# Spare transposes and products on TensorE at three waits of a Nyström attention and expert kernel

## The chip, the cores and the metric

The kernel runs on one core of one Trainium2 chip. The metric is the device time of one execution in microseconds (us); times of several runs are given as their median. Durations of single instructions come from one profiled execution, with times counted from the start of its span.

The engines are called here by what the profile calls them: PE is TensorE's matmuls, PEld its weight loads, DVE is VectorE, ACT is ScalarE, POOL is GpSimd, SP is the engine that issues DMAs.

## What is computed

The input x has 16 batches of 1024 rows with 256 columns. Each batch goes through two residual sublayers:

```
x = x + layernorm(attention(layernorm(x)))
x = x + layernorm(experts(layernorm(x)))
```

The attention has 16 heads of 16 columns and 64 landmarks, the means of 16 neighbouring rows:

```
kernel1 = softmax(Q K_l^T)        # 1024 x 64
kernel2 = softmax(Q_l K_l^T)      # 64 x 64
kernel3 = softmax(Q_l K^T)        # 64 x 1024
SV  = (kernel1 @ iterative_inv(kernel2)) @ (kernel3 @ V)
out = SV @ w_proj
```

`iterative_inv` makes six rounds of a polynomial iteration for the inverse. The expert layer reconstructs each batch with eight small networks, picks the expert with the least squared error for the whole batch, and adds that expert's two-layer adapter to a common linear layer. All of this is in 32-bit floats.

## The kernel before

Each batch is cut into stages that are Python generators: `stage_a` (normalized and transposed rows, Q, K, V, and kernel3 @ V), `stage_p` (kernel2 and its inverse, times the result of `stage_a`), `stage_c` (kernel1 times that, the projection, the first residual), `stage_d1` (the eight reconstructions and the choice) and `stage_d2` (the chosen adapter and the second residual). The stages of neighbouring batches are interleaved by hand: the string `ORDER` says which of five streams emits its next piece, and the engines' instruction streams keep that order. Each engine runs its instructions strictly in the order in which they were emitted, and waits on semaphores for others.

PSUM, the memory that matmuls write, is used as four buffers of two banks. `two_banks` (L135) hands out the next one by the string `PAIRS`, again by hand; the first instruction that writes a buffer waits until the last one that reads its former contents is done.

The places that the change touches:

- **`spare` (L154)** issues matmuls of a constant tile of ones, in bf16, into a buffer whose contents are overwritten later. In the kernel before, `turned_rows` calls it for the last batch (20 products of 512 columns) and `stage_d2` for the last batch (16 of 512).
- **Row maxima of kernel3, in `stage_a`.** `max_of` computes scores and takes their maxima on DVE (L556, eight reductions in batch 0); L624 and `in_parts` (L340 to L344) join them and split them into three bf16 parts in `maxima3`; L632 transposes that on PE into the PSUM tile `pm`, and L634 turns it into `mrow`. Then `weights` adds the negative maxima by a product (L567), computes the scores again (L578), and ACT takes the exponential (L588); `times_v` (L604) multiplies with V, and L612 and L614 sum up over the steps. Between these, DVE computes statistics and normalized rows of the next batch (L363, L347, L390). L743 and L751 belong to `stage_p`: the column sums of kernel2 and their maximum.
- **The end of `stage_a`.** L653 transposes the sums `ut` into the tile `pu`; L658 and L660 divide. In `stage_p`, POOL copies the result (L767), and the inverse's products follow in `product` (L698, tiles `pkv`, `pxl`, `pxq`), between them ACT copies (L780) and DVE operations (L762, L771, L783, L787); L793 copies the result into the block matrix `w_bd`.
- **Maxima of kernel1, in `stage_c`.** `max_of` (L823 on PE, L831 on DVE, split by POOL at L340 to L344) fills `maxima`; `max_rows` transposes it by four transposes (L853) into a PSUM tile `pm`, and ACT copies that to `mt` (L855). `weights` computes scores (L862), subtracts the maxima by a product with `mt` (L870) and takes exponentials (L880); `weighted` multiplies with `w_bd` (L891); `projected` is L926.
- **`turned_rows` (L396)** transposes normalized rows by L404, which ACT copies out at L405. At the end of the work, these come from batch 14's `stage_d1` while batch 15 is in `stage_c`.

`ident_b` is a 128x128 identity in bf16, `ones_b` a 128x128 tile of ones in bf16; both are made once at the start.

Of the kernel before, what the change touches and what calls it, by code (L numbers as in the profile page):

```python
# [16 lines left out]
P = 128  # L17
# [63 lines left out]
def kernel(  # L81
# [17 lines left out]
    nc = tc.nc  # L99
# [9 lines left out]
    E, _, R = wa_down.shape  # L109
# [13 lines left out]
    def middle(ap, n):  # L123

        return ap.unsqueeze(1).to_broadcast([ap.shape[0], n, ap.shape[1]])
# [4 lines left out]
    def rows32(p):  # L130
        return slice(32 * p, 32 * p + 32)
# [3 lines left out]
    def two_banks(shape, name, dtype=F32):  # L135
        return ps2 if isinstance(ps2, Nothing) else ps2.tile(shape, dtype, tag=f"ps2_{next(pairs)}", name=name)

    LAST = NB - 1
# [12 lines left out]
        return work.tile(shape, F32, tag=tag, name=name, bufs=bufs)  # L151


    def spare(dst, n):  # L154

        for _ in range(n):
            nc.tensor.matmul(dst, lhsT=ones_b, rhs=middle(ones_b, 4), start=True, stop=True)

    live = [{} for _ in range(NB)]

# [76 lines left out]
    ident_b = const.tile([P, P], BF16, name="ident_b")  # L237
    nc.vector.tensor_copy(ident_b, ident)
    ones_b = const.tile([P, P], BF16, name="ones_b")
# [115 lines left out]
    def go(name, follows):  # L355
        return name, follows
# [37 lines left out]
    def turned_rows(b, at, xn_of, xt):  # L394

        for h in range(NT // 4):  # L396
            yield go((at, b, "xt", h), [(at, b, "xn", h)])
            xn = xn_of(h)
            pt = two_banks([P, NC, 4, P], f"pt_{at}{b}_{h}")
            if b == LAST:  # L400
                spare(pt[:, 0], 20 if h == 0 else 0)
            for j in range(4):
                for k in range(NC):
                    nc.tensor.transpose(pt[:, k, j, :], xn[:, j, k * P : (k + 1) * P], ident)  # L404
            nc.scalar.copy(xt[:, :, h * 512 : (h + 1) * 512], pt.rearrange("p k j c -> p k (j c)"))  # L405
# [40 lines left out]
    def stage_a(b):  # L446
# [13 lines left out]
        for i, scale in enumerate((HD**-0.5, 1.0)):  # L460
            for c in range(NC):
# [8 lines left out]
                dst = (qt, kt)[i]  # L470
                pq = rows_split(f"pq_{b}_{i}_{c}")
                f0 = i * D + c * P
                for k in range(ND):
                    for g in range(4):
                        nc.tensor.matmul(  # L475
                            pq[g // 2][:, g % 2, 0 : N // 4],
                            lhsT=wqkv_sb[rows32(g), k, f0 : f0 + P],
                            rhs=turned[rows32(g), k],
                            start=(k == 0),
                            stop=(k == ND - 1),  # L480
# [11 lines left out]
        for t0 in range(0, NT, 4):  # L492
# [5 lines left out]
            for k in range(ND):  # L498
                for g in range(4):
                    nc.tensor.matmul(  # L500
                        pv[g // 2][:, g % 2, 0:D],
                        lhsT=turned[rows32(g), k, t0 // 4, :],
                        rhs=wqkv_sb[rows32(g), k, 2 * D : 3 * D],
                        start=(k == 0),
                        stop=(k == ND - 1),
# [123 lines left out]
        in_parts(nc.vector, lambda q: maxima3[:, :, q * NC : (q + 1) * NC], most, most)  # L629
        yield go(("a", b, "mrow"), [("a", b, "mcol")])  # L630
        pm = two_banks([P, P], f"pm3_{b}", BF16)
        nc.tensor.transpose(pm, maxima3.rearrange("x p j -> x (p j)"), ident_b)  # L632
        mrow = small.tile([P, NC, P], BF16, tag="mrow", name=f"mrow_{b}", bufs=1)
        nc.vector.tensor_tensor(mrow, middle(pm, NC), last(minus_pick, P), ALU.mult)  # L634
# [14 lines left out]
            ("a", b, "u"), [("a", b, "ut", i) for i in steps] + ([("p", b - 2, "kv0")] if b >= 2 else [])  # L649
        )  # L650
        pu = two_banks([P, NC, PC, 32], f"pu_{b}")
        for c in range(NC):
            nc.tensor.transpose(  # L653
                pu[:, c].rearrange("x p d -> x (p d)"), ut[:, c].rearrange("x r l -> x (r l)"), ident
            )
# [143 lines left out]
    def stage_c(b):  # L799
# [49 lines left out]
        def max_rows(n):  # L849

            pm = two_banks([P, 512], f"pm_{b}_{n}", BF16)
            for t in range(4):
                nc.tensor.transpose(pm[:, t * P : (t + 1) * P], maxima[:, t, :], ident_b)  # L853
            mt = work.tile([P, 512], BF16, tag="mt", name=f"mt_{b}_{n}", bufs=1)
            nc.scalar.copy(mt, pm)  # L855
            return mt
# [87 lines left out]
        max_of(0, 2)  # L944
        yield before_rows(0)
        mt = max_rows(0)
        po = None
        for n in range(NW):
            for c in range(NC):
                yield before_weights(n, c)  # L950
                es = weights(n, c, mt)
                if n + 1 < NW:
                    yield before_max(n + 1, 2 * c)
                    max_of(n + 1, 2 * c)
                elif c == 0:
                    yield from added(n - 1, *po)
                yield before_weighted(n, c)
                if c == 0:
                    svn = buf4k("yc", [P, ND, P], f"svn_{b}_{n}")
                weighted(n, c, es, svn)  # L960
            flat = svn.rearrange("p k c -> p (k c)")
            nc.vector.transpose(flat, flat)  # L962
            if n + 1 < NW:
                yield before_rows(n + 1)
                mt = max_rows(n + 1)
            po = yield from projected(n, svn)
# [150 lines left out]
    def stage_d2(b):  # L1117
# [3 lines left out]
        if b == LAST:  # L1121
            spare(pa[:, 0, :].rearrange("p (j c) -> p j c", j=4), 16)
# [62 lines left out]
    def streams():  # L1185
        ffn, alone = [stage_d1, stage_d2], NB - 2
        return [
            *(chain([stage]) for stage in (stage_a, stage_p, stage_c)),
            chain(ffn, [b for b in range(NB) if b != alone]),
            chain(ffn, [alone]),  # L1190
        ]
# [68 lines left out]
```

## Time and profile before

| what | us |
|---|---|
| median of 3 runs | 1929.07 (1927.91 to 1931.19) |
| the profiled execution's own time | 1931.63 |
| its span, first to last instruction | 1929.7 |
| PE busy | 1836.1 |
| DVE busy | 1511.2 |
| ACT busy | 1131.7 |
| POOL busy | 211.9 |

The profile is of one execution. Busy time of PE counts a matmul from its start to its modelled end, so overlapping matmuls are counted once. PEclk is the granted clock of TensorE as a share of its full speed; in the view that cuts the span into 40 slices it is given in tenths. The chain of waits goes back from the last instruction, at each step to what released it. In the timeline, each line has the start, the length, the engine, the line of the code, the operation, the tiles, the count, and in brackets how long the engine stood idle before and who ended that. In the view by stretches, each line has the stretch, its length, then busy time and number of instructions of PE, PEld, DVE, ACT and POOL, then PEclk, the DMA engines' share and GB/s.

### The profile page before, as it was taken

The page shows a single profiled execution, that of the slowest core. Times are in us where ns is not written, and L with a number is a line of the kernel's source. Part 1 is how long each engine was busy: PE and PEld are TensorE (multiplying, and loading weights), DVE is VectorE, ACT ScalarE, POOL GpSimd, SP SyncE. Part 2 cuts the span into 40 slices and gives each one's busy share as a digit, 9 for nine tenths or more (in the row PEclk, how much of TensorE's full clock was granted, in tenths as well). Part 3 has the DMA queues.
Part 4 walks back from the last instruction along what each step waited for, and adds up shares of the span by engine and source line. Part 5 has one row for each costly group of instructions (what it writes and reads, how often), then busy time and mean ns, then how long its engine had stood idle before and what let it go on. Part 6 is the DMA issues. An engine that isn't in the chain of part 4 may idle for free.

```text
span 1929.7 us, 81483 instructions
## 1 busy us (share of the span) xinstructions
PE 1836.1 (95%) x37175; PEld 1260.4 (65%) x37175; DVE 1511.2 (78%) x2805; ACT 1131.7 (59%) x2434; POOL 211.9 (11%) x423
## 2 busy tenths in 40 slices
PE   6789999999999999999999999999999999999898
PEld 5767678567585766858667575766758475756444
DVE  7687878877879787888878888788787877786664
ACT  1244755574846657474674847557484666666575
POOL 1001001001010100101101010100111010010101
PEclk9899999999999999999999999999999999999899
DMA  9011011102011110201102020110201110010101
GB/s 205 2 25 25 3 29 47 24 7 68 6 47 23 51 24 7 69 4 49 25 18 57 7 68 2 51 25 7 68 6 47 24 51 3 17 36 18 35 4 49
DMA packets 65767, 64.30 MB, mean 33 GB/s; under 512 B 9244, under 2 KB 65424, under 8 KB 65424
## 3 DMA queue, kind: packets, MB, share of 16 engines
q1 hardware_dynamic: 65424, 59.11, 11.8%
q8 instruction: 291, 4.77, 1.0%
q14 instruction: 52, 0.43, 0.1%
HBM read 42.32 MB, written 16.78 MB: 31 GB/s over the span
## 4 chain that ended last, share of the span: by engine, by line
PE 74%; ACT 11%; DVE 11%; issue 2%; POOL 1%; DMA 0%; SPq 0%; DVEq 0%; POOLq 0%; ACTq 0%
PE pq L475 12%; PE ph L999 10%; PE pr L1029 7%; PE pv L500 6%; ACT df L1040 6%; PE pf L1158 5%; PE po L926 4%; PE psv L891 4%; PE psct L862 3%; PE psc L823 3%; PE psm L547 3%; PE pxl L698 3%; DVE mx L556 2%; PE psc L578 2%; PE pxq L698 2%
## 5 line engine op out<-in xcount | busy, mean ns | idle before, releaser
L1040 ACT ACTIVATE df<-df,bd_sb 128x512 f32<-128x512 f32 x512 | 362.4, 711 | 72.0 <-DVE df L1037 71.9
L1037 DVE TENSOR_TENSOR df<-pr,xt_d 128x1024 f32<-128x1024 f32 x256 | 297.0, 1215 | 52.3 <-PE pr L1029 39.0
L475 PE MATMUL pq<-xa,wqkv_sb 32*128 32x256 f32 x4096 | 243.4, 381 | 15.1 <-DVE xa L390 15.0
L1029 PE MATMUL pr<-ht,wd_sb 64*64 64x512 f32 x2048 | 240.8, 597 | 1.7 <-ACT ht L1007 1.2
L999 PE MATMUL ph<-xt_d,wd_sb 128*128 128x512 f32 x512 | 236.5, 604 | 1.9 <-DVE most L831 1.2
L475 PEld LDWEIGHTS pq<-xa,wqkv_sb 32*128 32x128 f32 x4096 | 218.1, 186 | 27.7 <-DVE xa L390 15.0
L556 DVE TENSOR_REDUCE mx<-psm 128x2 f32<-128x1024 f32 x128 | 149.6, 1217 | 32.5 <-PE psm L547 32.2
L999 PEld LDWEIGHTS ph<-xt_d,wd_sb 128*128 128x128 f32 x512 | 92.1, 189 | 116.1 <-issue 95.1
L880 ACT ACTIVATE e<-psct 128x1024 f32<-128x1024 f32 x128 | 124.0, 1022 | 66.4 <-PE psct L870 66.2
L831 DVE TENSOR_REDUCE most<-psc 128x16 f32<-128x1024 f32 x128 | 150.2, 1216 | 13.5 <-PE psc L823 10.3
L1029 PEld LDWEIGHTS pr<-ht,wd_sb 64*64 64x64 f32 x2048 | 68.3, 132 | 126.1 <-issue 61.6
L588 ACT ACTIVATE e<-psc 128x1024 f32<-128x1024 f32 x128 | 123.0, 1026 | 31.4 <-PE psc L578 30.9
L1007 ACT ACTIVATE ht<-ph,bd_sb 128x1024 f32<-128x1024 f32 x64 | 70.9, 1108 | 105.3 <-PE ph L999 105.2
L926 PE MATMUL po<-wproj_sb,svn 32*128 32x256 f32 x2048 | 128.4, 381 | 2.1 <-DVE svn L962 0.9
L500 PE MATMUL pv<-wqkv_sb,xa 32*128 32x256 f32 x2048 | 125.6, 379 | 0.1
L926 PEld LDWEIGHTS po<-wproj_sb,svn 32*128 32x128 f32 x2048 | 108.1, 185 | 20.5 <-DVE df L1037 9.5
L1158 PE MATMUL pf<-wbase_sb,xt_d 128*128 128x256 f32 x512 | 119.1, 386 | 0.0
L500 PEld LDWEIGHTS pv<-wqkv_sb,xa 32*128 32x128 f32 x2048 | 109.8, 185 | 7.1 <-ACT kt L483 0.9
L1158 PEld LDWEIGHTS pf<-wbase_sb,xt_d 128*128 128x128 f32 x512 | 94.6, 190 | 22.2 <-issue 10.6
L787 DVE SCALAR_TENSOR_TENSOR xw<-xw,pxq 128x640 f32<-128x640 f32 x96 | 69.4, 723 | 50.4 <-PE pxq L698 50.2
L891 PEld LDWEIGHTS psv<-w_bd,e 128*32 128x32 f32 x8192 | 77.3, 109 | 34.2 <-issue 11.9
L483 ACT ACTIVATE qt<-pq 128x512 f32<-128x512 f32 x64 | 34.7, 595 | 107.7 <-PE pq L475 107.7
(185 smaller groups left out, 3090.0 us busy)
## 6 DMA issues: line engine op xcount, KB each, us to landing
x<-in_L_attn_x_dram SPq DMA_DIRECT2D x16, 1024.0 KB
xa<-in_L_attn_x_dram SPq DMA_DIRECT2D x60, 256.0 KB
out_dram<-y_d SPq DMA_DIRECT2D x30, 512.0 KB
wqkv_sb<-in_L_attn_w_qkv_dram SPq DMA_DIRECT2D x12, 256.0 KB
wup<-in_L_ffn_Wa_up_dram SPq DMA_DIRECT2D x30, 64.0 KB
xa<-in_L_attn_x_dram SPq DMA_DIRECT2D x8, 128.0 KB
wproj_sb<-in_L_attn_w_proj_dram SPq DMA_DIRECT2D x4, 256.0 KB
out_dram<-y_d SPq DMA_DIRECT2D x4, 256.0 KB
```

The lines of the kernel that those rows point to most:

```text
L475: nc.tensor.matmul(pq[g // 2][:, g % 2, 0 : N // 4], lhsT=wqkv_sb[rows32(g), k, f0 : f0 + P], rhs=turned[rows32(g), k], start=(k == 0), st ...
L500: nc.tensor.matmul(pv[g // 2][:, g % 2, 0:D], lhsT=turned[rows32(g), k, t0 // 4, :], rhs=wqkv_sb[rows32(g), k, 2 * D : 3 * D], start=(k == 0),
L556: nc.vector.tensor_reduce(mx3[:, n, q : q + 2], psc[g], X, ALU.max)
L831: nc.vector.tensor_reduce(mx[:, t0 : t0 + 2, 2 * g : 2 * g + 2].rearrange("x t p j -> x p t j"), psc[g].rearrange("x p t c (r l) -> x p t ...
L880: nc.scalar.activation(e, psc[g], AF.Exp)
L891: nc.tensor.matmul(psv[rows32(g), j // 2, col : col + 2 * (HD + 1)], lhsT=es[p // 2][:, p % 2, g * P + 32 * j : g * P + 32 * j + 32], rhs= ...
L926: nc.tensor.matmul(po[g // 2][:, g % 2, 0:D], lhsT=svt[rows32(g), k, :], rhs=wproj_sb[rows32(g), k, :], start=(k == 0), stop=(k == ND - 1),)
L999: nc.tensor.matmul(ph[:, n, :], lhsT=wd1_sb[:, k, 2 * i : 2 * i + 2, :].rearrange("p e h -> p (e h)"), rhs=xt[:, k, n * 512 : (n + 1) * 51 ...
L1029: nc.tensor.matmul(pr[to, r, :], lhsT=wd2_sb[half, i, k * P + 64 * f : k * P + 64 * f + 64], rhs=ht[half, cols], start=True, stop=True,)
L1037: nc.vector.tensor_tensor(df, pr, middle(xt[:, k, cols], 2), ALU.subtract)
L1040: nc.scalar.activation(df[:, r, :], df[:, r, :], AF.Square, bias=bd2_sb[:, e, k : k + 1], accum_out=part[:, e, k * NW + n : k * NW + n + 1],)
L1158: nc.tensor.matmul(banks[j // 2][:, j % 2, :], lhsT=xt[:, k, cols], rhs=wbase_sb[:, k, :], start=False, stop=(j % 2 == 1 and k == NC - 1),)
```

## The change

Three places get instructions on PE whose results nobody reads. Batch 0's `pm` tile gets 25 transposes of the identity ahead of its one real transpose. Batch 0's `pu` tile gets 16 products of 256 columns ahead of its two real transposes. The last batch's first `pm` tile in `stage_c` gets 40 transposes of the identity, all into the first 128 columns, ahead of its four real ones. The real instructions write the same places afterwards. `spare` gets an argument for the number of 128-column repeats, with the old value as default. Everything else, with `ORDER` and `PAIRS`, stays.

```diff
-    def spare(dst, n):
+    def spare(dst, n, wide=4):
 
         for _ in range(n):
-            nc.tensor.matmul(dst, lhsT=ones_b, rhs=middle(ones_b, 4), start=True, stop=True)
+            nc.tensor.matmul(dst, lhsT=ones_b, rhs=middle(ones_b, wide), start=True, stop=True)
+
+    def spare_turns(dst, n):
+
+        for _ in range(n):
+            nc.tensor.transpose(dst, ident_b, ident_b)
...
         pm = two_banks([P, P], f"pm3_{b}", BF16)
+        if b == 0:
+            spare_turns(pm, 25)
         nc.tensor.transpose(pm, maxima3.rearrange("x p j -> x (p j)"), ident_b)
...
         pu = two_banks([P, NC, PC, 32], f"pu_{b}")
+        if b == 0:
+            spare(pu.rearrange("x c p d -> x c (p d)"), 16, 2)
         for c in range(NC):
...
             pm = two_banks([P, 512], f"pm_{b}_{n}", BF16)
+            if (b, n) == (LAST, 0):
+                spare_turns(pm[:, 0:P], 40)
             for t in range(4):
                 nc.tensor.transpose(pm[:, t * P : (t + 1) * P], maxima[:, t, :], ident_b)
```

## The prediction

> **What bounds the kernel now.** I read the page first: busy shares, slices, chain of waits.
>
> ```profile
> PE 1836.1 (95%) x37175; PEld 1260.4 (65%) x37175; DVE 1511.2 (78%) x2805; ACT 1131.7 (59%) x2434; POOL 211.9 (11%) x423
> ...
> PEclk9899999999999999999999999999999999999899
> ...
> PE 74%; ACT 11%; DVE 11%; issue 2%; POOL 1%; DMA 0%; SPq 0%; DVEq 0%; POOLq 0%; ACTq 0%
> ```
>
> TensorE is busy 95% of the span and is 74% of the chain that ends last. Its granted clock is at full nearly throughout (mean 0.99); only slices 2 and 38 are marked down, and the three edits lie in those two. So nothing large can move: the change can only give back time that TensorE spends at half clock there.
>
> Second view: busy time and clock by stretch. I narrowed the stretches until the clock (PEclk, the first number behind PE's and the other engines' busy times) switched at their borders. It fell at 49.60, 66.66, 117.86, 1759.67 and 1786.98 us and rose at 56.42, 76.90, 121.28, 1763.09 and 1800.63. All these differ by whole multiples of 3.41 us, so I cut the trace into windows of 3.41 us with borders there. PE's busy time is the number behind the window's length:
>
> ```profile
> 46.18:49.60 3.42, 0.30 (x2) 0.00 (x0) 3.42 (x4) 0.00 (x0) 0.00 (x0) 1.00 0.25 44
> 49.60:53.01 3.41, 1.51 (x22) 1.38 (x26) 2.72 (x12) 0.00 (x0) 0.00 (x0) 0.50 0.00 0
> 53.01:56.42 3.41, 3.41 (x63) 3.08 (x60) 2.85 (x12) 2.11 (x3) 1.39 (x3) 0.50 0.02 5
> ...
> 63.25:66.66 3.41, 1.09 (x60) 0.93 (x60) 3.38 (x6) 0.31 (x1) 0.00 (x0) 1.00 0.00 0
> 66.66:70.07 3.41, 1.25 (x18) 0.85 (x22) 1.52 (x5) 0.00 (x0) 0.29 (x1) 0.50 0.00 0
> 70.07:73.49 3.42, 1.66 (x51) 1.45 (x49) 1.52 (x2) 0.00 (x0) 0.00 (x0) 0.50 0.00 0
> 73.49:76.90 3.41, 3.41 (x77) 3.02 (x72) 1.58 (x2) 0.69 (x1) 0.00 (x0) 0.50 0.02 5
> ...
> 349.97:353.38 3.41, 2.09 (x116) 1.51 (x118) 1.18 (x4) 0.00 (x0) 0.00 (x0) 1.00 0.02 5
> 1756.26:1759.67 3.41, 2.05 (x110) 1.67 (x112) 2.58 (x13) 3.38 (x7) 1.20 (x2) 1.00 0.02 5
> ...
> 1783.57:1786.98 3.41, 1.67 (x51) 1.48 (x55) 2.15 (x5) 2.81 (x10) 1.02 (x3) 1.00 0.19 66
> 1786.98:1790.39 3.41, 1.24 (x24) 0.94 (x16) 3.31 (x7) 0.00 (x0) 0.28 (x1) 0.50 0.94 271
> 1790.39:1793.81 3.42, 0.00 (x0) 0.00 (x0) 3.42 (x4) 0.00 (x0) 0.24 (x1) 0.50 0.36 126
> 1793.81:1797.22 3.41, 2.27 (x12) 1.03 (x16) 3.14 (x14) 0.59 (x1) 2.08 (x5) 0.50 0.00 0
> 1797.22:1800.63 3.41, 3.41 (x48) 2.51 (x40) 3.32 (x12) 1.94 (x2) 1.33 (x2) 0.50 0.02 5
> ```
>
> Read each row with the clock of the next. At full clock, a window with 2.05 us or less of PE is followed by half clock; one with 2.09 is not. At half clock, 2.27 us do not bring it back; full windows (3.37 and more in this trace) do. This is my working rule: a fall below about 2.07 us in a window, a rise somewhere between 2.3 and 3.4.
>
> Third view: the timeline. PE stands idle from 46.48 to 50.98 (for VectorE's eight maxima and the split into three parts), from 64.70 to 67.84 (for L614's last sum), and from 1788.22 to 1794.95 (VectorE's four L831, then GpSimd's split).
>
> **The spares, instruction by instruction.** Start to length, us:
>
> ```profile
> 1794.95 0.61 PE L853 MATMUL pm<-ident_b,maxima 128*128 128x128 bf16 x4 [6.74 <-POOL maxima L342]
> ...
> 1811.50 0.40 PE L853 MATMUL pm<-ident_b,maxima 128*128 128x128 bf16 x4
> ...
> 1848.43 4.49 PE L157 MATMUL pt_d<-ones_b 128*128 128x512 bf16 x20
> ```
>
> One bf16 transpose of 128x128 takes 0.22 us at full clock, 0.31 at half, but four take 0.40 and 0.61: each further one adds (0.40-0.22)/3 = 0.06 at full and (0.61-0.31)/3 = 0.10 at half. A spare product of 512 columns adds (4.49-0.38)/19 = 0.216; one of 256 columns I estimate at half of that, 0.108 (below by 0.06, the transpose of 128 columns; above by 0.216).
>
> **Edit 1, 25 transposes at the row maxima of batch 0.** Their PSUM buffer was last read by the fifth L556 (ends 46.43), so they start at 46.48 and take 0.22 + 24 x 0.06 = 1.7 us, to 48.1, well inside the wait. Window 46.18:49.60 then holds 0.30 + 1.7 = 2.0 us. That is between 1.67 and 2.05, which both fell; the clock falls at 49.60 as before. Gain taken: 0. If it just holds, the next window still has only some 1.5 us and falls at 53.01; then the first score step (L567 and L578, 2.1 us at half, 1.07 at full) gains about 1.0. The upper end, no half clock at all up to 56.42: two such steps are 2.1 us shorter, of which VectorE's statistics, which end at 56.1 and stand ahead of the reduction L751 that frees a score buffer, let through 1.3. Loss: 0, unless the spares pass 50.98. Ends: 0 to -1.3.
>
> **Edit 2, 16 products at the sums of batch 0.** Their buffer was read by an exponential that ended before the last products of L604, so they start at 64.70 and take 0.25 + 15 x 0.108 = 1.9, to 66.6; the wait ends at 67.84. Window 63.25:66.66 gets 1.09 + 1.9 = 3.0 and holds. The next one, 66.66:70.07, has 1.25 or less and falls at 70.07. So one window is won: the transposes pu take 0.44 (L653 in later batches) for 0.69, pkv 0.78 (L698) for 1.34, together 0.8 us. But the rise stays at 76.90, so work that comes 0.8 us earlier runs 0.8 us longer at half clock: it is worth 0.4 at the end. Taken: -0.4. Upper end, no half clock from 66.66 to 76.90: 0.25 for pu, 0.56 each for pkv and pxl, and from pxl's end to pxq's end 3.2 us at half against about 2.4 (copy 0.69, q 0.69, pxq 0.78, hops), together -2.2. Loss 0.
>
> **Edit 3, 40 transposes at the last batch's first maxima.** The buffer's last reader is the first of the four L831, which ends at 1790.10. The clock is already at half (window 1783.57:1786.98, where PE waited from 1784.78 to 1786.52, before the spares). So 0.31 + 39 x 0.10 = 4.2 us, 1790.15 to 1794.4 at the latest; the wait ends at 1794.95, so they are hidden with 0.6 to spare. Window 1790.39:1793.81 becomes full, and the clock rises at 1793.81 in place of 1800.63. Window 1793.81:1797.22 then holds the last spares (0.3), pm 0.40, L862 1.1, L870 0.4 and most of L698 (0.7): 2.7, so the clock stays. What it is worth: up to pxq PE is done about 1 us earlier, but then VectorE's xn_d of L347 is late next; it runs on regardless, its first four pieces to 1799.17, its last four to 1800.80. So the first eight L404 end at about 1799.6 (1800.82 before), ScalarE's copy L405 at 1800.65, its four copies L793 (1.03) at 1801.65, and the products L891, which need them, start at 1801.7 in place of 1802.88. Taken: -1.2. From there the chain goes on through PE, ACT and DVE with no transfer that does not depend on it, so it arrives at the end. Ends: 0 (the clock does not rise) to -1.5.
>
> [...] In this trace transposes do count for the clock: window 1797.22:1800.63, after which it rose, holds 1.71 us of the fp32 transposes L404, and window 1851.83:1855.25, which held with 2.14 us, 1.04 us of them. [...] No row shows a long run of bf16 transposes.
>
> **Sum.** 0 - 0.4 - 1.2 = -1.6 us. The profiled execution took 1931.63 (span 1929.7 and 1.9 around it), so 1930.0; it stands 2.56 above the median of the runs, 1929.07. The median becomes 1927.5. All other instructions and their order stay; 65 transposes and 16 products are 81 of 37175.
>
> **Rivals.**
> *All three stretches keep full clock* (the windows lie differently, or the rule is milder): -1.3 - 2.2 - 1.5 = -5.0, 1924.1. For it: the rule's bound lies within 0.1 us of edit 1's window, and the windows need not lie at the same place in every execution. Against: after spare 1 ends at 48.1 PE has 0.27 us of work up to 51.77, more than one whole window; the chain from 67.84 to 76 waits for VectorE and ScalarE about half the time.
> [...]
> *Slower: spares to one and the same PSUM place do not overlap*, each then taking its whole 0.31 or 0.22 us. Edit 3 would need 3.66 us for its first 12 (rise at 1793.81) and 28 x 0.22 = 6.2 more, to 1800.0 for 1794.95: +5.1, less 1.2; edits 1 and 2 would overrun by about 1 each and win it back by the clock. About +3.9: 1933.0. It decides from 0.15 us for each transpose at half clock; the rows show 0.10. Against: the 20 products of L157, all to one place, overlap (0.216 for a length of 0.38).
>
> **Numbers.** 0.2% is 3.9 us, about what a measurement of this kernel can tell from no change. Forecast 0.60, no counting 0.14, all kept 0.20, slower 0.06. Forecast and no counting lie within 0.2%; only the whole of the first rival's gain passes it. So faster 0.20, same 0.74, slower 0.06. The range goes from all kept, 1924.1, to somewhat above the median with nothing gained, since the runs of before alone spread from 1927.91 to 1931.19: 1930.3.
>
> **What would show it.** Spares from 46.48, 64.70 and 1790.15, ended by 48.2, 66.7 and 1794.4; clock at half from about 50 to 56 still; later fall in the second stretch by one window; rise near 1794 in the third, and L891 some 1.2 us sooner after L831. Wrong if the full clock holds through 51.77 or 70.1, if the third stretch is at half until 1800, or if pm starts later than its maxima.

## The result and the profile after

The changed kernel takes 1957.18 us (median of 4 runs, 1954.14 to 1959.27), the kernel before 1930.13 beside it (4 runs, 1927.91 to 1932.79): a ratio of 1.0139, 95% interval 1.0126 to 1.0151. That is 27 us slower. The forecast was 1927.5, the range ended at 1930.3; the direction was wrong too.

The page of the changed kernel, for the lines shown of before, and the line of the instruction queue (which reads 291, 4.77, 1.0% in the kernel before). Line numbers differ from kernel to kernel, since the edits add lines: L891 of before is L902 here.

```profile
span 1957.3 us, 81645 instructions
...
PE 1853.5 (95%) x37256; PEld 1271.6 (65%) x37256; DVE 1512.3 (77%) x2805; ACT 1132.2 (58%) x2434; POOL 211.6 (11%) x423
...
PEclk9899999999999999999999999999999999999899
...
q8 instruction: 292, 4.78, 1.0%
```

The 81 spares are there and nothing else is new; busy time of DVE, ACT and POOL is as before. The clock row is the same digit for digit. PE is busy 17 us more, of which the spares are 7.9, and idle 10 us more. (The chain of waits breaks off after a few per cent of the span in this profile and says nothing.)

The three places, in the timeline of the changed kernel (start, length):

```profile
46.99 1.55 PE L162 MATMUL pm<-ident_b 128*128 128x128 bf16 x25
51.49 0.22 PE L639 MATMUL pm<-ident_b,maxima 128*128 128x128 bf16 x1 [2.95 <-DVE maxima L347]
...
64.52 1.92 PE L157 MATMUL pu<-ones_b 128*128 128x256 bf16 x16
67.73 0.44 PE L662 MATMUL pu<-ident,ut 128*128 128x128 f32 x2 [1.29 <-DVE ut L619]
69.15 0.78 PE L707 MATMUL pkv<-k2w 64*64 64x80 f32 x32 [0.98 <-POOL k2w L776]
...
1815.82 4.42 PE L162 MATMUL pm<-ident_b 128*128 128x128 bf16 x40 [2.48 <-DVE most L840]
1820.62 0.61 PE L864 MATMUL pm<-ident_b,maxima 128*128 128x128 bf16 x4 [0.38 <-POOL maxima L347]
```

All spares end inside their waits, with 2.95, 1.29 and 0.38 us left. So the places themselves cost nothing. Comparing the start of each VectorE instruction with its start in the trace of before, the changed kernel is 0.8 us ahead at 126 us, 1.3 behind at 154, 7 behind at 536, 14 at 1234 and 25 at 1590: the loss is spread over the 1660 us in which the two programs are the same.

Who PE waited for, summed over the trace, by the waits view (total, times, longest, us); only the largest rows that end in "issue" are shown. First the changed kernel, then the kernel before:

```profile
PE psv L902 <- issue: 11.3, 9, 1.9
PE pxl L707 <- issue: 4.6, 7, 1.3
PE psc L583 <- issue: 3.0, 3, 1.2
PE pq L480 <- issue: 2.8, 5, 0.9
PE pxq L707 <- issue: 2.6, 2, 1.8
```

```profile
PE psv L891 <- issue: 5.3, 5, 2.3
PE put L604 <- issue: 1.2, 2, 0.9
PE psc L578 <- issue: 1.2, 1, 1.2
PE pxq L698 <- issue: 1.0, 1, 1.0
```

"issue" is a wait for nothing that the profile shows: no semaphore, no engine. It falls inside runs of equal products, as in these lines of the changed kernel's timeline:

```profile
133.59 0.43 PE L752 MATMUL pcs<-k2w,ones 64*64 64x256 f32 x1
134.62 0.66 PE L752 MATMUL pcs<-k2w,ones 64*64 64x256 f32 x7 [0.60 <-issue]
135.21 1.24 PE L902 MATMUL psv<-w_bd,e 128*32 128x34 f32 x121
138.35 0.27 PE L902 MATMUL psv<-w_bd,e 128*32 128x34 f32 x7 [1.90 <-issue]
```

The run of 128 products psv (kernel1 times `w_bd`) is cut after 121, the run of eight pcs (column sums of kernel2) after one. From the last matmul before the first cut to the last before the second, there are 256 of PE's instructions (7 pcs and 121 psv, each a weight load and a matmul). So I numbered all recorded instructions of PE, in order of start, and summed the gaps of over 0.3 us (less 0.1) between starts by number modulo 256. One residue, so one place in the block of 256, stands out, 192: 22 gaps of 16.3 us in the kernel before, 44 gaps of 39.1 us in the changed one; an average residue has 6 gaps of 2.2 us. The queue "instruction" moves 291 packets of 16 KB in the kernel before: 74678 recorded instructions of PE make 256.6 for each packet. The first theory, **blocks**, follows: PE's instructions are fetched in blocks of 256; where PE uses up a block faster than the next arrives, it stands at the block's end; 81 spares put each later instruction up to 162 places further along, and the ends fell on denser stretches. Its rivals: **clock** (the spares' windows start more half clock elsewhere: the trace has three such windows more between 121 and 1759 us, after 138.5, 1230.8 and 1524.3) and **order** (the spares hold up the first batch and the engines fall out of step).

### The profile page after: what moved, and what is told of

It is laid out like the page before. It is cut to its first block, busy times and chain, and to the rows that moved or that the text cites. A ratio compares the mean times of both kernels' runs of the same rounds, so it can differ in the third digit from the quotient of the medians.

```text
span 1957.3 us, 81645 instructions
## 1 busy us (share of the span) xinstructions
PE 1853.5 (95%) x37256; PEld 1271.6 (65%) x37256; DVE 1512.3 (77%) x2805; ACT 1132.2 (58%) x2434; POOL 211.6 (11%) x423
## 5 line engine op out<-in xcount | busy, mean ns | idle before, releaser
L891 ACT ACTIVATE e<-psct 128x1024 f32<-128x1024 f32 x128 | 124.1, 1023 | 78.0 <-PE psct L881 77.7
L902 PEld LDWEIGHTS psv<-w_bd,e 128*32 128x32 f32 x8192 | 77.4, 108 | 40.7 <-issue 19.0
L902 PE MATMUL psv<-w_bd,e 128*32 128x34 f32 x8192 | 85.9, 197 | 15.0 <-issue 11.3
```

The source lines that it names most:

```text
L891: nc.scalar.activation(e, psc[g], AF.Exp)
L902: nc.tensor.matmul(psv[rows32(g), j // 2, col : col + 2 * (HD + 1)], lhsT=es[p // 2][:, p % 2, g * P + 32 * j : g * P + 32 * j + 32], rhs= ...
```

## The experiments

All ratios are against the kernel before on the same chip; the changed lines are shown against before or against the changed kernel, as said.

**The shift alone, by 82 places** (against before; the same edit with 128, 64 and 116 products follows below):

```diff
                 pq = rows_split(f"pq_{b}_{i}_{c}")
+                if (b, i, c) == (0, 0, 0):
+                    for _ in range(41):
+                        nc.tensor.matmul(pq[0][:, 0, 0:1], lhsT=ones_b, rhs=ones_b[:, 0:1], start=True, stop=True)
```

> The kernel before with 41 products of one column, read by nobody, ahead of its first product (PE is idle there until 14.97 us), and none of the three edits. They shift PE's later instructions by 82 places, as the first two edits do (41 weight loads and 41 matmuls or transposes). Theory 'blocks': PE's instructions come in blocks of 256 (291 fetches of 16 KB for 74678 recorded instructions), PE stands where a dense stretch crosses from one block to the next, and the shift moves the crossings onto worse places: 22 such stalls of 16.3 us together before, 44 of 39.1 us after. It expects +22 to +28 us. Theory 'clock': the slowdown is half clock in other windows, started by the spares: 0 +- 2 us. Theory 'order': the spares delay the first batch and the engines fall out of step: 0 +- 2 us.

Measured 1960.88 us, ratio 1.0157 (1.0140 to 1.0174), +31 us. There is no spare at any of the three places, and the slowdown is there. The timeline of this kernel shows the cuts at the same instructions as the changed kernel's:

```profile
138.52 0.43 PE L751 MATMUL pcs<-k2w,ones 64*64 64x256 f32 x1
139.55 0.66 PE L751 MATMUL pcs<-k2w,ones 64*64 64x256 f32 x7 [0.60 <-issue]
140.13 1.24 PE L899 MATMUL psv<-w_bd,e 128*32 128x34 f32 x121
143.55 0.27 PE L899 MATMUL psv<-w_bd,e 128*32 128x34 f32 x7 [2.18 <-issue]
```

"Clock" and "order", as they were put above, are refuted as the cause of the loss.

**The whole change, filled up to a whole block** (the changed kernel, and `range(87)` in the lines above):

> The changed kernel with 87 more products of one column ahead of its first product, so that from batch 0 on PE's instructions stand 256 places later than before (41 + 87 pairs), one whole block. Theory 'blocks': the time before, less what the clock gives back, so -3 to +1 us against before. Theories 'clock' and 'order': still +27 us, since all three edits are there.

Measured 1930.91, ratio 1.0004 (0.9993 to 1.0014). All three edits are there, 174 more instructions are there, and the loss is gone.

**A whole block and nothing else** (before, `range(128)`):

> The kernel before with 128 such products at its start: 256 places, one whole block. Theory 'blocks': 0 +- 2 us. If the products themselves cost something (a cold queue, their own fetch), it shows here: more than +2 us.

Measured 1932.10, ratio 1.0009 (0.9999 to 1.0018); just outside the 2 us of the expectation, with an interval that reaches down to 0. The cuts stand again where the kernel before has them: in both timelines the run psv near 136 us is cut into 34 and 94. First the kernel before, then shift256:

```profile
134.97 0.51 PE L891 MATMUL psv<-w_bd,e 128*32 128x34 f32 x34
136.36 1.02 PE L891 MATMUL psv<-w_bd,e 128*32 128x34 f32 x94 [0.89 <-issue]
...
135.86 0.51 PE L899 MATMUL psv<-w_bd,e 128*32 128x34 f32 x34
136.97 1.02 PE L899 MATMUL psv<-w_bd,e 128*32 128x34 f32 x94 [0.60 <-issue]
```

**The third edit alone** (the changed kernel without the first two):

> The third edit alone: 40 transposes at 1790 us, nothing in batch 0. Theory 'blocks': no shift up to 1790 us, so no slowdown there; behind it the shift is 80 places for the last 140 us, which hold 4.2 us of the 16.3 us of stalls in the kernel before: -3 to +2 us. Theory 'clock': the dips before 1790 are gone with the first two edits, the clock rises near 1794: -1 us. Theory 'order': 0.

Measured 1930.29, ratio 1.0004 (0.9994 to 1.0015). No loss without a shift ahead of the dense stretches. What it does at its own place is read below.

**Half a block and nearly a whole one** (before, `range(64)` and `range(116)`):

> The kernel before with 64 products of one column at its start, a shift of 128 places, half a block. Theory 'blocks': the time goes with the place in the block, not with the number of products. With the rule that a block's end may be passed 3.5 us after the end before it was reached, applied to the trace of before, the stalls sum to 54 us for this shift, against 14 for none and 42 for 82 (counted in the traces: 16 and 39): +33 to +43 us. The rival, that each added product costs, would give 64/41 of shift82's +31, +48 us.

> 116 products at the start, a shift of 232 places. Theory 'blocks': the same sum is 26 us for this shift, 12 more than for none: +8 to +18 us, though it has nearly three times the products of shift82. The rival, that each added product costs, would give 116/41 of +31, +88 us.

Measured 1978.69, ratio 1.0245 (1.0226 to 1.0263), +48 us, with 64 products, and 1942.39, ratio 1.0059 (1.0040 to 1.0077), +12 us, with 116. The first is above the blocks' range and just what a price for each product would give; taken alone it would have spoken for the rival. The second decides: 116 products cost a quarter of what 64 cost, where a price for each asks for +88. The time goes with the place in the block.

**The pace of the fetch, at the start and at a quiet place** (before; 512 products at the start, 640 at `pu` of batch 0; the second's lines):

```diff
         pu = two_banks([P, NC, PC, 32], f"pu_{b}")
+        if b == 0:
+            for j in range(640):
+                nc.tensor.matmul(pu[rows32(j % 4), 0, 0, 0:1], lhsT=ones_b[:, 0:32], rhs=ones_b[:, 0:1], start=True, stop=True)
```

> 512 products of one column with 32 columns of weights at the start, 1024 instructions, four whole blocks, in PE's idle time before 14.97 us. The 128 products psv with 32 columns of weights take 1.3 us in the trace, so a block of 256 instructions could run in about 1.3 to 2.6 us. Theory 'blocks': after the first blocks PE stands at each block's end, and a block takes 3.3 to 3.8 us whatever is in it. Without a limit on the fetch: no idle time between the products, 5 to 10 us for all.

> 640 products of one column with 32 columns of weights, over the four column groups in turn as psv has them, ahead of batch 0's transposes pu at 64.7 us: 1280 instructions, five whole blocks, at a place where the DMA engines have nothing else to do (share 0.00 in the kernel before; 1.10 where fetch_pace ran). 128 such products take 1.3 us in psv, so 6.5 us without a limit. Theory 'blocks': after the first block PE stands at each block's end, and from end to end a block takes 3.3 to 3.9 us.

The first missed its number: the products ran at 28 ns each, so a block took 3.55 us by itself, and its ends came 5.4 and 8.9 us apart, with waits of 0.36, 1.82 and 5.38 us, while the input's transfers kept the DMA engines full (share 1.10 to 1.13). So beside other transfers on the DMA engines a block took much longer to arrive. The second shows the pace alone (the times of these two, 1939.43 and 1941.68 us, are of one execution each and are not used):

```profile
64.90 1.17 PE L659 MATMUL pu<-ones_b 128*32 128x1 bf16 x128 [0.33 <-issue]
68.63 1.18 PE L659 MATMUL pu<-ones_b 128*32 128x1 bf16 x128 [2.56 <-issue]
72.08 1.18 PE L659 MATMUL pu<-ones_b 128*32 128x1 bf16 x128 [2.27 <-issue]
75.81 1.18 PE L659 MATMUL pu<-ones_b 128*32 128x1 bf16 x128 [2.54 <-issue]
79.26 1.05 PE L659 MATMUL pu<-ones_b 128*32 128x1 bf16 x112 [2.27 <-issue]
```

Equal pieces of exactly 128 products, 256 instructions, each done in 1.18 us and followed by a wait; from start to start 3.73, 3.45, 3.73 and 3.45, 3.6 on the mean. One block in 3.6 us is the most that PE got here. The products psv want 256 instructions in 1.3 us, so whether they fit depends on how long ago the block before was begun.

The traces also hold the packets of the queue "instruction" with their times, and these tie the waits to the fetch. Each of the 13 traces has exactly as many packets as block ends (places 192 modulo 256): 291 in the kernel before, 292 in the changed one. At the quiet place the packets begin at 66.01, 69.75, 73.21 and 76.92 us, 1.1 us after the first product of each piece, and last 0.9 to 1.3 us; PE goes on 1.2 to 1.4 us after their end. There, each of these packets began only after PE had begun the block before. In the changed kernel's trace that holds for 218 of 291 packets, and 38 of its 44 cuts end 1.2 to 1.6 us after the end of a packet. The cut at 138.35 in the changed kernel is of the same kind: PE enters the block at 134.62, the packet runs from 135.68 to 136.80, and PE goes on at 138.35. Beside the full DMA engines the packets began 2.7 and 6.1 us after PE had entered the block, in place of 1.1, and themselves took 1.23 and 1.35 us: what became longer there is mainly the time before a packet starts.

**The first two edits, each alone** (the changed kernel without the others):

> The first edit alone, 25 transposes, a shift of 50 places from 47 us on. Theory 'blocks': the sum of stalls by the 3.5 us rule is 30 us for a shift of 50, 14 for none: +13 to +20 us. That an added product costs as such (25/41 of shift82's +31): +19. Theory 'clock': 0 to -1.

> The second edit alone, 16 products, a shift of 32 places from 65 us on. Theory 'blocks': the sum is 19 us for a shift of 32, so +5, less 0.4 from the clock: +2 to +8 us. That an added product costs as such: 16/41 of +31, +12. Theory 'clock': -0.4 to -0.8.

Measured 1945.30, ratio 1.0077 (1.0051 to 1.0103), and 1937.70, ratio 1.0045 (1.0033 to 1.0058): against 1928.15 beside them +17 and +10 us. The first is in its range, the second above. Both places, hidden in their waits, cost many times what their clock could give. That the two add up to the change's +27 is no rule: shifts do not add, as 128 and 232 places show.

**A version for both** (the changed kernel without its first edit; 112 products at the start make the second edit's shift a whole block, 18 at the last batch move its ends):

```diff
                 pq = rows_split(f"pq_{b}_{i}_{c}")
+                if (i, c) == (0, 0) and b in (0, LAST):
+                    for _ in range(112 if b == 0 else 18):
+                        nc.tensor.matmul(pq[0][:, 0, 0:1], lhsT=ones_b, rhs=ones_b[:, 0:1], start=True, stop=True)
```

> Edits 2 and 3 without edit 1, with 112 products of one column at the start, so that the shift after edit 2 is 128 pairs, one whole block; and 18 such products ahead of the last batch's first product, a shift of 36 places from there. Theory 'blocks': the same sum finds 3.7 us less stall behind 1568 us with that shift; 18 pairs cost at most 0.5 us. With the clock's -0.4 (edit 2) and -1.2 (edit 3): -2 to -6 us against before. If the clock's gain was nothing: -2 to -4.

Measured 1929.42 beside 1930.48, ratio 0.9993 (0.9983 to 1.0003). The -2 to -6 us that were expected did not come: an advantage of 2 us is not excluded, but it isn't shown. With 14.4 us of gaps at block ends in its profile, against 12.4 to 16.3 in the kernels without a net shift, the last batch's 3.7 us did not come out.

The gaps at residue 192 and the measured times together:

| kernel | shift, places | gaps there, us (count) | time against before, us |
|---|---|---|---|
| before | 0 | 16.3 (22) | |
| shift256 | 256 | 12.4 (20) | +2.6 |
| the change, whole blocks | 256 | 13.0 (19) | +1.4 |
| second edit alone | 32 | 20.9 (24) | +9.6 |
| first edit alone | 50 | 24.4 (31) | +17 |
| the change | 82 | 39.1 (44) | +27 |
| shift82 | 82 | 38.2 (43) | +31 |
| shift128 | 128 | 50.7 (46) | +48 |
| shift232 | 232 | 20.3 (22) | +12 |

The gaps are those of the one profiled execution, the times are medians; that matters most for shift232, whose runs spread from 1934.49 to 1943.75 us and whose profile is of one of 1936.82.

The gaps make 22.8 of the change's 27 us. The clock makes little of the rest, by an estimate. Each of the three new half-clock windows does follow a window with such a gap (135.11:138.53 holds 1.52 us of PE and the gap of 1.90), as does a fourth, after 1831.54, and 3.41 us at half clock cost at most 1.7 each. But the edits also took half clock away: over the whole trace PE is busy at half clock for 31.0 us, of which 4.4 are hidden spares, against 24.9 before. If half of such time is lost, the net loss is an estimated 0.8 us. For the other shifts the gaps make only a third to three quarters of the loss. The count leaves out gaps below 0.3 us and block ends at which PE waited for an engine anyway, and I did not separate these from what other engines do with the delay: that part stays open.

## Why the prediction was wrong, step by step

- *"Loss: 0, unless the spares pass 50.98"* and *"Loss 0"* for the second edit, and in the sum *"All other instructions and their order stay; 65 transposes and 16 products are 81 of 37175"*. **This is the step that failed**, and with it the premise that "nothing large can move". I priced the spares by the time in which they run and took their number for nothing. Each run alone, the first two edits cost 17 and 10 us by the places by which they shift what follows, 50 and 32, although the waits at which they run hide them entirely. The page of before had the sign of it, 291 instruction packets for PE's instructions, and the waits view had 5.3 us of psv waiting for "issue"; neither entered the sum.
- *The slower rival*, spares that do not overlap, did not happen: 25 transposes took 1.55 us (worked out: 1.7), 16 products 1.92 (1.9), 40 transposes 4.42 (4.2). The right sign had a mechanism that I did not name.
- *Edit 1's clock.* Forecast: falls at 49.6 as before. In the changed kernel the window 46.37:49.78 held with 2.17 us of PE, and only one window, 53.20 to 56.61, ran at half. The windows stood 0.2 us later and PE's start 0.5 us later than in the trace of before, so more of PE's work fell into that window. The prediction had named this ("If it just holds"), but took the other case; its sign of being wrong, full clock through 51.77, came true.
- *The working rule* (a fall below 2.07 us of PE in a window) fits the trace of before and does not carry over. In the changed kernel 998.69:1002.10 kept the full clock with 1.67 us of PE, in the first edit alone 46.70:50.12 kept it with 1.48; in the whole-block kernel 1793.09:1796.50 lost it with 2.28. So PE's busy time in these windows does not by itself decide the clock, and a forecast for edit 1's window, 0.1 us from the bound, could only be right or wrong by luck.
- *Edit 2's clock.* Right: the fall came one window later, at 70.26 for 66.66, with pu at 0.44 and pkv at 0.78 as worked out, pxl at 1.34. By 126 us the changed kernel was 0.8 us ahead of before, one execution against another, where 0.4 was forecast.
- *Edit 3.* Right, and best seen where nothing is shifted. The third edit alone, by windows (length, PE's busy time, and PEclk as the first number behind the engines), then its timeline:

```profile
1786.30:1789.71 3.41, 1.95 (x19) 1.95 (x19) 3.41 (x4) 0.00 (x0) 0.00 (x0) 0.50 0.78 261
1789.71:1793.13 3.42, 3.04 (x32) 2.58 (x29) 3.28 (x10) 0.00 (x0) 1.12 (x4) 0.50 0.02 5
1793.13:1796.54 3.41, 2.50 (x50) 1.47 (x49) 3.24 (x13) 2.53 (x3) 2.08 (x4) 1.00 0.00 0
```

```profile
1787.76 4.42 PE L162 MATMUL pm<-ident_b 128*128 128x128 bf16 x40 [2.48 <-DVE most L836]
1792.56 0.61 PE L860 MATMUL pm<-ident_b,maxima 128*128 128x128 bf16 x4 [0.38 <-POOL maxima L347]
...
1795.95 1.32 PE L409 MATMUL pt_d<-ident,xn_d 128*128 128x128 f32 x8 [0.91 <-DVE xn_d L352]
...
1799.32 1.30 PE L898 MATMUL psv<-w_bd,e 128*32 128x34 f32 x128
```

  The window full of bf16 transposes brought the clock back at 1793.13, VectorE's xn_d is what PE waits for next, as named, and from pm to psv there are 6.76 us where the kernel before has 1794.95 to 1802.88, 7.93: 1.2 us less, as forecast. Its whole time does not show it, so that the 1.2 us arrive at the end, as the prediction says, is not shown; its interval reaches from 1.2 us below before to 2.9 above.
- *"No counting", 0.14.* In the third edit alone PE's 3.04 us in the window 1789.71:1793.13 above are bf16 transposes but for the last 0.03 us, and the clock was full from 1793.13 on, so here bf16 transposes did count for the clock. Where the rise lies stays open: in shift256 a window with 2.71 us (117.42:120.83) did not bring the clock back, and neither did a full one (1796.78:1800.19).
- *The sum of -1.6 us* for the clock alone, with the shift filled up: +1.4 us, interval -1.4 to +2.7. So -1.6 is just excluded, and no gain is shown; against shift256, which has the same shift and no spares, it is 1.2 us less, within both intervals.

## What to carry to other kernels

Where PE is busy nearly all the time with small instructions (95% of the span and 37175 products here), the number of instructions ahead of a dense stretch can itself be a parameter (82 places cost 27 and 31 us here): before pricing an edit by its duration, count by how many places it moves PE's later instructions, and look in the trace for waits for "issue" that repeat every 256 (here 44 gaps at one place of 256 in the changed kernel, 6 at an average one). An edit that adds or takes away PE instructions is better compared with its count filled up to a whole block at an idle place, as here, where +27 us became +1.4. The kernel before happened to stand at the best place of the block that was tried: each of the five shifts by less than a block that were made at the start or in batch 0 (32, 50, 82, 128 and 232 places) lost.

## What was not expected of the hardware

At the quiet place (DMA share 0.02) PE's instructions arrived at no more than 256 in 3.6 us, 14 ns each, while PE needed 4.6 ns each for small products (256 in 1.18 us). Beside full DMA engines (share 1.10 to 1.13), block ends came 5.4 and 8.9 us apart. And a wait of 1.90 us at a block's end, the only one in its window, was followed by half clock in the 3.41 us from 138.5 us on in the changed kernel; one of 1.74 us at 998.9 was not.
